# A graph network in two layers: the first node tables as a software pipeline, with one difference on GpSimd and the loads on three queues

## The chip, the cores and the metric

The kernel runs on one core of a Trainium2 chip. A core has five engines that run side by side, each through its own instructions in order: PE (TensorE, matrix products into PSUM), DVE (VectorE), ACT (ScalarE), POOL (GpSimd) and SP (SyncE, which here only issues transfers). An instruction that waits for another engine holds up everything behind it on its own. ACT and POOL can issue transfers too. The time is microseconds on the device, from start to end of one execution. It is the median of several executions.

## The reference, cut to what matters

There are 6250 nodes with 128 channels and 200,000 edges, sorted by `dst`. Two layers of attention over the edges follow each other, each with a residual and a layer norm.

```python
# layer 0: a score for each edge, a softmax over the edges of one src
hij = concatenate([x[src], x[dst]], -1)
e = leaky_relu(hij @ w, 0.2) @ a
att = exp(e) / segment_sum(exp(e), src)[src]
x = layernorm(x + segment_sum(x[src] * att, dst))
# layer 1: four heads, scores from two projections, sum into src, elu
s = leaky_relu(H_s[:, src] + H_t[:, dst]); s = exp(s - max(s))
agg = scatter_add(src, s / (denom[src] + eps) * H[dst]) + x @ residual_projection
x = layernorm(x + elu(agg))
```

The change concerns only the start of layer 0: `hij @ w` is `x[src] @ w_top + x[dst] @ w_bottom`, so both products are made once for each node (the node tables) and then picked for each edge.

## The kernel before

The 6250 nodes make NB = 49 blocks of 128. The edges are sorted into NB x NB buckets by the block of their `src` and of their `dst`; each bucket has 128 slots. The work runs in three stages.

**Score stage** (`score_edges`). It holds all that the change touches.
- Constants come first, and `load_ids(0)` (L556 to L565) loads the source and destination numbers of the first seven windows of edges: fourteen transfers on SP's queue, seven for `src` and then seven for `dst`.
- `find_slots(j)` (from L596) is a generator that finds the slots of the edges of destination block j. Each `next` on it issues one portion, eleven portions in all. In this document they are calls one to eleven. (1) For a chunk's first j, `split_ids` takes the ids apart on DVE and asks for the next chunk's ids; then ACT repeats one part along a new axis (`repeat`, L606). (2) DVE compares (`soh`, L612). (3) PE adds up with a stair matrix (L619), ACT copies the sum (`earlier`, L621) and repeats two more parts. (4) Two `count`s, each a group of matmuls into one PSUM tile (L629, L631) and a DVE product from it (L638). (5) Three more counts, two folds (L653), a reduction to `ranks` (L656), and an ACT spread of half the ranks (L661). (6) Two DVE products `vst` (L670). (7) A DVE comparison `at` (L676), the second ACT spread. (8) PE places the first half (L681), DVE compares the second. (9) PE places the second half. (10) DVE takes the slots to `cb` and `cols` (L698, L699). (11) PE transposes, ACT copies to `rb` (L704), SP writes `rows_jm` and `rows_im` to DRAM (L706, L707).
- The node tables are made for blocks b = 0 to 48 (L720 to L758). PE transposes the block of x (L745), ACT copies it to `xt` (L747), PE multiplies (`tables`, L729) into 128x260 values in PSUM. Then `split3` (L474 to L481) writes them as three bf16 parts to `pq3`: ACT rounds (`high`, L477), DVE subtracts (L479, tile `pqr`), ACT rounds the rest (L480), DVE subtracts again (`low`, L481). Transposes run one block ahead of the products; the four operations of `split3` come in a row. x comes in chunks of seven blocks into three buffers, on SP's queue. All PSUM tiles of this loop, those of `count` among them, come from one pool "u" of four.
- In the same loop three searches start at blocks 0, 12 and 24, and `find_more` moves each running search on by one portion after every second block.
- Behind it the pair loop goes over all 49 x 49 pairs of blocks (7 chunks of 7 for each j). It fetches slot rows, makes one-hot matrices of them on DVE (L793), multiplies them with `pq3` (L817), and takes the scores from PSUM on DVE (L827). The searches of the later j run between. Its buffers follow those of the table loop, in memory and in PSUM.

**Layer 0** and **layer 1** (`bucketed`) gather and sum with one-hot matrices (L1050, L1080; L1217, L1249).

The order on each engine is the order in which the program text issues the instructions; no planner changes it. POOL works only on constants at the start of the stages.

Of the kernel before, what the change touches and what calls it, by code (L numbers as in the profile page):

```python
# [8 lines left out]
F32 = mybir.dt.float32  # L9
# [3 lines left out]
AF = mybir.ActivationFunctionType  # L13
OP = mybir.AluOpType
AX = mybir.AxisListType

P = 128
# [457 lines left out]
def split3(nc, pool, hi, mid, lo, v, shape, name):  # L475

    nc.scalar.activation(hi, v, AF.Copy)  # L477
    r = pool.tile(shape, F32, name=name)
    nc.vector.tensor_tensor(r, v, hi, op=OP.subtract)  # L479
    nc.scalar.activation(mid, r, AF.Copy)  # L480
    nc.vector.tensor_tensor(lo, r, mid, op=OP.subtract)  # L481


def score_edges(tc, keep, x, src, dst, w0, a0, rows_jm, rows_im):
# [4 lines left out]
    nc = tc.nc  # L489
    N, C = x.shape  # L490
    (E,) = src.shape
    NB = -(-N // P)
    LAST = N - (NB - 1) * P
    NI = -(-NB // 2) * 2
    WT, starts = windows(N, E, NB)
    CX = C + 2
    CH = 7
    chunks = [(c, min(c + CH, NB)) for c in range(0, NB, CH)]
    NC = len(chunks)
    AHEAD = 3  # L500
# [7 lines left out]
    with ExitStack() as pools:  # L508
# [22 lines left out]
        ident = fc.tile([P, P], F32, name="ident")  # L531
# [5 lines left out]
        w0_sb = fc.tile([P, 2, CX], F32, name="w0_sb")  # L537
# [10 lines left out]
        part = ALPHA / (1.0 - ALPHA)  # L548
# [6 lines left out]
        ids, parts = {}, {}  # L555

        def load_ids(b):
            if b < NC:
                c0, c1 = chunks[b]
                ids[b] = [fi.tile([P, CH, WT], I32, name=f"ids{k}") for k in range(2)]  # L560
                for to, flat in zip(ids[b], (src, dst)):
                    for j in range(c0, c1):
                        nc.sync.dma_start(
                            to[:, j - c0, :], flat[starts[j] : starts[j] + WT * P].rearrange("(p t) -> p t", t=WT)
                        )  # L565

        def split_ids(b):


            load_ids(b + 1)  # L570
            c0, c1 = chunks[b]
            n = c1 - c0
            got = []
            for k, number in enumerate(ids.pop(b)):
                number = number[:, :n].rearrange(flat2)
                hl = fi.tile([P, 2, CH, WT], BF16, name=f"hl{k}")
                for h, (by, op) in enumerate(((7, OP.arith_shift_right), (P - 1, OP.bitwise_and))):
                    tmp = fi.tile([P, CH * WT], I32, name="tmp")
                    nc.vector.tensor_single_scalar(tmp[:, : n * WT], number, by, op=op)
                    nc.vector.tensor_scalar(  # L580
                        hl[:, h, :n].rearrange(flat2), tmp[:, : n * WT], 1.0, None, op0=OP.add
                    )
                got.append(hl)
            here = fi.tile([P, CH, WT], BF16, name="here")
            nc.vector.tensor_tensor(
                here[:, :n],
                got[1][:, 0, :n],
                iota_1[:, c0:c1, None].to_broadcast([P, n, WT]),
                op=OP.is_equal,
            )  # L590
            nc.vector.tensor_reduce(counts[:, b : b + 1], here[:, :n].rearrange(flat2), axis=AX.X, op=OP.add)
            nc.vector.tensor_tensor(got[0][:, 0, :n], got[0][:, 0, :n], here[:, :n], op=OP.mult)  # L592
            parts[b] = got[0][:, 0], got[0][:, 1], got[1][:, 1]
# [115 lines left out]
        finding, pa = [], []  # L709

        def find_more():
            for f in list(finding):
                if next(f, finding) is finding:
                    finding.remove(f)


        load_ids(0)
        pqp = pools.enter_context(tc.tile_pool(name="pq", bufs=1))
        pq3 = pqp.tile([P, NB, 2, 3, CX], BF16, name="pq3")
        with (  # L720
            tc.tile_pool(name="n0", bufs=3) as n0,
            tc.tile_pool(name="n0u", bufs=4, space=bass.MemoryType.PSUM) as n0u,
        ):
            pa[:] = [n0u]
            ahead, turned = iter(range(AHEAD)), []

            def tables(b, xt):
                mm = n0u.tile([P, 512], F32, name="u")[:, : 2 * CX].rearrange("p (w c) -> p w c", c=CX)
                nc.tensor.matmul(mm, xt, w0_sb, start=True, stop=True)  # L729
                split3(nc, n0, pq3[:, b, :, 0, :], pq3[:, b, :, 1, :], pq3[:, b, :, 2, :], mm, [P, 2, CX], "pqr")  # L730

            for c0, c1 in chunks:
                xc = n0.tile([P, CH, C], F32, name="xc")
                full = min(c1, NB - 1) if LAST < P else c1
                if full < c1:
                    nc.vector.memset(xc[:, full - c0, :], 0.0)
                    nc.sync.dma_start(xc[:LAST, full - c0, :], x[full * P :, :])
                if full > c0:
                    nc.sync.dma_start(
                        xc[:, : full - c0, :], x[c0 * P : full * P, :].rearrange("(b p) c -> p b c", p=P)  # L740
                    )
                for b in range(c0, c1):

                    tp = n0u.tile([P, 512], F32, name="u")[:, :P]
                    nc.tensor.transpose(tp, xc[:, b - c0, :], ident)  # L745
                    xt = n0.tile([P, P], F32, name="xt")
                    nc.scalar.activation(xt, tp, AF.Copy)  # L747
                    turned.append((b, xt))
                    if b > 0:
                        tables(*turned.pop(0))  # L750
                    if b % 12 == 0:
                        finding.extend(find_slots(j) for j in [next(ahead, None)] if j is not None)
                    if b % 2 == 0:
                        find_more()
            tables(*turned.pop(0))
            assert next(ahead, None) is None
            while finding:
                find_more()  # L758

# [40 lines left out]
        for k, (j, c) in enumerate(order):  # L800
# [7 lines left out]
            rows = loaded.pop(k)  # L808
            c0, c1 = chunks[c]
            for i0 in range(c0, c1, 3):  # L810
                n = min(3, c1 - i0)
                u = pa[0].tile([P, 512], F32, name="u")[:, : 3 * CX].rearrange("p (n c) -> p n c", c=CX)
                for d in range(n):
                    i = i0 + d
                    for w, b in ((0, i), (1, j)):
                        for s in range(3):
# [4 lines left out]
                                start=(w == 0 and s == 0),  # L821
                                stop=(w == 1 and s == 2),
# [8 lines left out]
            tp = ft.tile([P, CH, P], BF16, name="tp")  # L831
# [504 lines left out]
@with_exitstack  # L1336
def kernel(ctx, tc, x, src, dst, w0, a0, w1, al, ar, wr, out):
    nc = tc.nc
    ctx.enter_context(tc.manual_schedule())
    NB = -(-x.shape[0] // P)  # L1340
    keep = ctx.enter_context(tc.tile_pool(name="keep", bufs=1))
    dram = ctx.enter_context(tc.tile_pool(name="slots_d", bufs=1, space=bass.MemoryType.DRAM))
    rows_jm = dram.tile([NB, 2, NB, P], BF16, name="rows_jm")
    rows_im = dram.tile([NB, 2, NB, P], BF16, name="rows_im")
    cols, ok, ex, den = score_edges(tc, keep, x, src, dst, w0, a0, rows_jm, rows_im)
    fits = nc.values_load(
        ok, min_val=0, max_val=1, skip_runtime_bounds_check_because="a product of two comparisons is 0 or 1"
    )
    with tc.If(fits == 1) as cmp:
        bucketed(tc, x, w1, al, ar, wr, out, cols, ex, den, rows_jm, rows_im)  # L1350
    with cmp.Else():
        any_edges(tc, x, src, dst, w0, a0, w1, al, ar, wr, out)
# [35 lines left out]
```

## Time and profile before

| | |
|---|---|
| median of three runs | 4135.72 us (4134.61 to 4139.05) |
| the profiled execution | 4133.56 us |
| its span, first to last instruction | 4131.8 us |
| mean granted PE clock over the span | 0.957 of full speed |
| busy: PE, DVE, ACT, POOL | 3637.4, 3385.6, 2238.6, 1.7 us |
| first node table matmul (L745), last `low` (L481) | 11.71, 152.27 us |
| first fetch of slot rows issued, first pair matmul (L817) | 152.76, 158.18 us |
| end of the score stage, about | 1682 us |

Times inside the profile count from the first instruction. Each row of the time order names the start, the duration, the engine, the line of the program, the operation, the tile that it writes and those that it reads with their shapes; in brackets stands how long the engine had been idle before it, and what it waited for. In the list of waits the columns are the waiting engine and line, what it waited for, the total in microseconds, how many times, and the longest. The granted clock is the share of full speed that TensorE was given.

### The profile page before, as it was taken

The numbers are of one execution on the slowest core, as the hardware profiler recorded it, in microseconds if no ns is written. First come the engines' busy times: TensorE is split into PE (matmuls) and PEld (weight loads), VectorE is DVE, ScalarE is ACT, GpSimd is POOL, SyncE is SP. The second block draws the span as 40 slices with busy tenths as digits, with TensorE's granted clock in tenths as the row PEclk, the third lists the DMA queues.
The fourth block names the chain that finished last, engine by engine and source line by source line (L and its number), as shares of the span: only waits on it lengthen the run. The fifth ranks groups of instructions, "written<-read, shape, count | busy, mean of one in ns | idle before, by whom it ended". The sixth has DMA issues, their size and how long they took to land.

```text
span 4131.8 us, 133418 instructions
## 1 busy us (share of the span) xinstructions
PE 3637.4 (88%) x55225; PEld 3463.4 (84%) x55225; DVE 3385.6 (82%) x11437; ACT 2238.6 (54%) x3384; POOL 1.7 (0%) x12
## 2 busy tenths in 40 slices
PE   5788899898889889499999999997999999999982
PEld 3588888888888888399999999996999999999972
DVE  5688888888888888588788888876888888888886
ACT  5456555555555554234434434436666766666653
POOL 0000000000000000000000000000000000000000
PEclk7899999999999999699999999997999999999995
DMA  1233333333333333222322222224444444444431
GB/s 31 74 110 110 105 103 110 108 106 101 114 106 106 99 114 117 78 83 78 82 79 78 79 82 78 79 71 135 133 134 132 135 134 136 129 134 135 135 96 50
DMA packets 300811, 423.28 MB, mean 102 GB/s; under 512 B 53094, under 2 KB 298660, under 8 KB 300196
## 3 DMA queue, kind: packets, MB, share of 16 engines
q1 hardware_dynamic: 299204, 414.19, 33.3%
q8 instruction: 438, 7.18, 0.7%
q14 instruction: 177, 1.45, 0.1%
q10 hardware_dynamic: 992, 0.46, 0.0%
HBM read 405.66 MB, written 8.87 MB: 100 GB/s over the span
## 4 chain that ended last, share of the span: by engine, by line
PE 60%; DVE 28%; ACT 6%; issue 2%; DMA 2%; SPq 0%; DVEq 0%; ACTq 0%
PE oj L1080 13%; PE agg L1249 12%; PE ye L1050 9%; PE he L1217 9%; PE u L817 7%; DVE junk L827 5%; DVE at L676 3%; DVE rows L793 3%; ACT spread L661 3%; DVE r L638 2%; DVE vst L670 2%; PE sm L619 2%; DVE z L1228 1%; PE sp L1175 1%; DVE r L653 1%
## 5 line engine op out<-in xcount | busy, mean ns | idle before, releaser
L817 PE MATMUL u<-pq,rows 128*128 128x130 bf16 x14406 | 914.7, 221 | 104.1 <-DVE junk L827 96.3
L817 PEld LDWEIGHTS <-rows 128*128 128x128 bf16 x14406 | 851.1, 98 | 122.1 <-issue 116.7
L1062 DVE TENSOR_SCALAR oh<-iota_b,dsts,ex 128x128 f32<-128x128 bf16 x2401 | 658.1, 340 | 144.3 <-PE oj L1080 106.0
L1249 PE MATMUL agg<-z,oh 128*128 128x132 f32 x4802 | 700.6, 287 | 70.9 <-DVE oh L1235 70.9
L1080 PE MATMUL oj<-yc,oh 128*128 128x128 f32 x4802 | 691.3, 284 | 3.3 <-ACT yc L1058 2.9
L1249 PEld LDWEIGHTS agg<-z,oh 128*128 128x128 f32 x4802 | 601.9, 193 | 72.5 <-issue 60.1
L1058 ACT ACTIVATE yc<-ye 128x512 f32<-128x512 f32 (+1 forms) x686 | 370.6, 543 | 538.3 <-PE ye L1050 532.1
L827 DVE SCALAR_TENSOR_TENSOR junk<-u,a_ext 128x130 bf16<-128x130 f32 x2401 | 544.8, 286 | 105.6 <-PE u L817 104.2
L1080 PEld LDWEIGHTS oj<-yc,oh 128*128 128x128 f32 x4802 | 596.2, 193 | 5.2 <-ACT yc L1058 4.0
L1050 PE MATMUL ye<-y,rows 128*128 128x128 bf16 x7203 | 519.5, 220 | 76.9 <-DVE rows L925 76.9
L1050 PEld LDWEIGHTS <-rows 128*128 128x128 bf16 x7203 | 465.5, 99 | 93.2 <-issue 59.2
L1228 DVE TENSOR_TENSOR z<-he,z 128x512 f32<-128x512 f32 (+1 forms) x686 | 424.6, 619 | 135.6 <-ACT z L1225 83.0
L1217 PE MATMUL he<-h,rows 128*128 128x128 bf16 x7203 | 519.0, 220 | 0.0
L835 ACT ACTIVATE oh<-tp 128x896 bf16<-128x896 bf16 x343 | 311.8, 909 | 336.5 <-PE tp L833 334.5
L1217 PEld LDWEIGHTS <-rows 128*128 128x128 bf16 x7203 | 443.8, 98 | 6.5
L1235 DVE TENSOR_TENSOR oh<-iota_b,cols 128x512 f32<-128x512 bf16 (+1 forms) x686 | 420.5, 613 | 0.0
L920 ACT ACTIVATE rows<-rows,minus_p 128x896 bf16<-128x896 bf16 x343 | 352.3, 1027 | 1.6 <-DMA rows<-rows_im 1.6
L661 ACT ACTIVATE spread<-ranks 128x2816 bf16<-128x2816 bf16 x98 | 249.3, 2544 | 168.2 <-DVE ranks L656 168.2
L921 ACT ACTIVATE rows<-rows 128x896 bf16<-128x896 bf16 x343 | 325.9, 950 | 10.9
L606 ACT ACTIVATE spread<-hl 128x2200 bf16<-128x2200 bf16 x147 | 292.8, 2024 | 39.6 <-DVE hl L592 39.6
L925 DVE TENSOR_SCALAR rows<-rows,part_f 128x896 bf16<-128x896 bf16 x686 | 301.8, 446 | 12.9 <-DMA rows<-rows_im 9.2
L1225 ACT ACTIVATE z<-score,neg_c 128x16 f32<-128x16 f32 (+1 forms) x686 | 184.3, 296 | 220.4 <-PE agg L1249 153.6
(158 smaller groups left out, 3701.9 us busy)
## 6 DMA issues: line engine op xcount, KB each, us to landing
rows<-rows_jm SPq DMA_DIRECT2D x1029, 224.0 KB
rows<-rows_im SPq DMA_DIRECT2D x686, 224.0 KB
res_d<-rs SPq DMA_DIRECT2D x7, 448.0 KB
res<-res_d SPq DMA_DIRECT2D x7, 448.0 KB
xc<-in_x_dram SPq DMA_DIRECT2D x6, 448.0 KB
out_dram<-o SPq DMA_DIRECT2D x6, 448.0 KB
rows_jm<-rb SPq DMA_DIRECT2D x98, 12.2 KB
rows_im<-rb SPq DMA_DIRECT2D x98, 12.2 KB
```

The costliest lines, as they stand in the source:

```text
L661: nc.scalar.activation(rx, ranks[:, h * WH : (h + 1) * WH, None].to_broadcast([P, WH, P]), AF.Copy)
L817: nc.tensor.matmul(u[:, d, :], rows[:, w, i - c0, :], pq3[:, b, w, s, :], start=(w == 0 and s == 0), stop=(w == 1 and s == 2),)
L827: nc.vector.scalar_tensor_tensor(junk, u[:, d, :], 0.0, a_ext, op0=OP.max, op1=OP.mult, accum_out=acc[:, i : i + 1])
L920: nc.scalar.activation(rows, rows, AF.Square, bias=minus_p)
L1050: nc.tensor.matmul(ye[:, k, :], oh[:, i0 + k - c0, :], y3[:, i0 + k, s, :], start=(s == 0), stop=(s == 2))
L1058: nc.scalar.activation(yc[:, :n], ye[:, :n], AF.Copy)
L1062: nc.vector.tensor_scalar(oh[:, k, :], iota_b, dsts[0][:, i : i + 1], ex[:, j, i : i + 1], op0=OP.is_equal, op1=OP.mult,)
L1080: nc.tensor.matmul(outs[j], oh[:, k, :], yc[:, k, :], start=(i == 0), stop=(i == NB - 1))
L1217: nc.tensor.matmul(he[:, k, :], oh[:, j0 + k - c0, :], h3[:, j0 + k, s, :], start=(s == 0), stop=(s == 2))
L1228: nc.vector.tensor_tensor(z[:, :n, :C].rearrange("p n (h d) -> p n h d", h=H), he[:, :n].rearrange("p n (h d) -> p n h d", h=H), z[:, :n, ...
L1235: nc.vector.tensor_tensor(oh[:, :n], iota_b[:, None, :].to_broadcast([P, n, P]), cols[:, j0 : j0 + n, 0, i : i + 1].to_broadcast([P, n, P] ...
L1249: nc.tensor.matmul(aggs[i], oh[:, k, :], z[:, k, :], start=(j == 0), stop=(j == NB - 1))
```

## The change

The order of the table loop is turned into steps. At step t each operation works on another block: rest (the first difference) on block t-4, the copy of the transposed block on t-1, the transpose on t, the product on t-2, high on t-3, middle on t-5, low on t-6. They are issued in this order in every step, 55 steps in all. The copy (`keep_turned`) moves from ACT to DVE, the second difference (`low`) from DVE to POOL. The PSUM pool "u" of four becomes one of three for the tables and one of a single tile for the counts. x is loaded into four buffers instead of three, on POOL's queue and one to two chunks ahead; the first chunk's `dst` ids come on ACT's queue. Searches start at steps 0, 14 and 28, and of the running searches those at an even place in the list move on at even steps, the others at odd ones.

```diff
--- before.py
+++ after.py
@@ -558,9 +558,9 @@
             if b < NC:
                 c0, c1 = chunks[b]
                 ids[b] = [fi.tile([P, CH, WT], I32, name=f"ids{k}") for k in range(2)]
-                for to, flat in zip(ids[b], (src, dst)):
+                for to, flat, queue in zip(ids[b], (src, dst), (nc.sync, nc.scalar if b == 0 else nc.sync)):
                     for j in range(c0, c1):
-                        nc.sync.dma_start(
+                        queue.dma_start(
                             to[:, j - c0, :], flat[starts[j] : starts[j] + WT * P].rearrange("(p t) -> p t", t=WT)
                         )
 
@@ -718,42 +718,72 @@
         pqp = pools.enter_context(tc.tile_pool(name="pq", bufs=1))
         pq3 = pqp.tile([P, NB, 2, 3, CX], BF16, name="pq3")
         with (
-            tc.tile_pool(name="n0", bufs=3) as n0,
-            tc.tile_pool(name="n0u", bufs=4, space=bass.MemoryType.PSUM) as n0u,
+            tc.tile_pool(name="n0", bufs=4) as n0,
+            tc.tile_pool(name="n0u", bufs=3, space=bass.MemoryType.PSUM) as n0u,
+            tc.tile_pool(name="n0c", bufs=1, space=bass.MemoryType.PSUM) as n0c,
         ):
-            pa[:] = [n0u]
-            ahead, turned = iter(range(AHEAD)), []
-
-            def tables(b, xt):
-                mm = n0u.tile([P, 512], F32, name="u")[:, : 2 * CX].rearrange("p (w c) -> p w c", c=CX)
-                nc.tensor.matmul(mm, xt, w0_sb, start=True, stop=True)
-                split3(nc, n0, pq3[:, b, :, 0, :], pq3[:, b, :, 1, :], pq3[:, b, :, 2, :], mm, [P, 2, CX], "pqr")
-
-            for c0, c1 in chunks:
+            pa[:] = [n0c]
+            rows, tps, xts, mms, rests = {}, {}, {}, {}, {}
+
+            def load_rows(c):
+                c0, c1 = chunks[c]
                 xc = n0.tile([P, CH, C], F32, name="xc")
                 full = min(c1, NB - 1) if LAST < P else c1
                 if full < c1:
-                    nc.vector.memset(xc[:, full - c0, :], 0.0)
-                    nc.sync.dma_start(xc[:LAST, full - c0, :], x[full * P :, :])
+                    nc.gpsimd.memset(xc[:, full - c0, :], 0.0)
+                    nc.gpsimd.dma_start(xc[:LAST, full - c0, :], x[full * P :, :])
                 if full > c0:
-                    nc.sync.dma_start(
+                    nc.gpsimd.dma_start(
                         xc[:, : full - c0, :], x[c0 * P : full * P, :].rearrange("(b p) c -> p b c", p=P)
                     )
                 for b in range(c0, c1):
-
-                    tp = n0u.tile([P, 512], F32, name="u")[:, :P]
-                    nc.tensor.transpose(tp, xc[:, b - c0, :], ident)
-                    xt = n0.tile([P, P], F32, name="xt")
-                    nc.scalar.activation(xt, tp, AF.Copy)
-                    turned.append((b, xt))
-                    if b > 0:
-                        tables(*turned.pop(0))
-                    if b % 12 == 0:
-                        finding.extend(find_slots(j) for j in [next(ahead, None)] if j is not None)
-                    if b % 2 == 0:
-                        find_more()
-            tables(*turned.pop(0))
-            assert next(ahead, None) is None
+                    rows[b] = xc[:, b - c0, :]
+
+            def part(b, s):
+                return pq3[:, b, :, s, :]
+
+
+            def turn(b):
+                tps[b] = n0u.tile([P, 512], F32, name="u")[:, :P]
+                nc.tensor.transpose(tps[b], rows.pop(b), ident)
+
+            def keep_turned(b):
+                xts[b] = n0.tile([P, P], F32, name="xt")
+                nc.vector.tensor_copy(xts[b], tps.pop(b))
+
+            def multiply(b):
+                mms[b] = n0u.tile([P, 512], F32, name="u")[:, : 2 * CX].rearrange("p (w c) -> p w c", c=CX)
+                nc.tensor.matmul(mms[b], xts.pop(b), w0_sb, start=True, stop=True)
+
+            def high(b):
+                nc.scalar.activation(part(b, 0), mms[b], AF.Copy)
+
+            def rest(b):
+                rests[b] = n0.tile([P, 2, CX], F32, name="pqr")
+                nc.vector.tensor_tensor(rests[b], mms.pop(b), part(b, 0), op=OP.subtract)
+
+            def middle(b):
+                nc.scalar.activation(part(b, 1), rests[b], AF.Copy)
+
+            def low(b):
+                nc.gpsimd.tensor_tensor(part(b, 2), rests.pop(b), part(b, 1), op=OP.subtract)
+
+            load_rows(0)
+            load_rows(1)
+            stages = ((rest, 4), (keep_turned, 1), (turn, 0), (multiply, 2), (high, 3), (middle, 5), (low, 6))
+            first = [0, 14, 28]
+            assert len(first) == AHEAD
+            for t in range(NB + 6):
+                if t % CH == 1 and 1 < t // CH + 2 < NC:
+                    load_rows(t // CH + 2)
+                for stage, lag in stages:
+                    if 0 <= t - lag < NB:
+                        stage(t - lag)
+                if t in first:
+                    finding.append(find_slots(first.index(t)))
+                for k, f in enumerate(list(finding)):
+                    if t % 2 == k % 2 and next(f, finding) is finding:
+                        finding.remove(f)
             while finding:
                 find_more()
```

## The prediction

> **What bounds the stage that the change touches.** I first cut the span into stages by the engines' busy time (columns: stretch, its length, then busy time and count for PE, weight loads, DVE, ACT, POOL, the granted clock, DMA share, GB/s).
>
> ```profile
> core 0: us, PE busy (x) PEld busy (x) DVE busy (x) ACT busy (x) POOL busy (x), PEclk, DMA share, GB/s
> 0.00:7.50 7.50, 0.00 (x0) 0.00 (x0) 3.29 (x17) 1.28 (x1) 0.95 (x8) 1.00 0.32 62
> 7.50:152.80 145.30, 82.62 (x561) 52.01 (x561) 79.18 (x154) 77.91 (x168) 0.00 (x0) 0.69 0.10 26
> 152.80:1682.00 1529.20, 1369.37 (x25558) 1281.69 (x25558) 1338.99 (x6096) 848.76 (x812) 0.00 (x0) 0.99 0.35 108
> ```
>
> Only the first 152.8 us are touched: node tables and the first three slot searches. No engine is full there: DVE 79 of 145 us, ACT 78, PE 83 at a clock of 0.69. So it is bound by waits, and all that can be won lies between 145 us and some 80. The pair stage after it can't begin earlier than its end (the first pair matmul, L817, starts at 158.18), so a microsecond saved here is one off the end. The waits of this stretch, longest first:
>
> ```profile
> DVE pqr L479 <- ACT pq L477: 39.0, 15, 6.3
> ACT pq L480 <- DVE pqr L479: 35.2, 49, 2.8
> ...
> DVE pq L481 <- ACT pq L480: 23.8, 49, 0.5
> ACT xt L747 <- PE u L745: 20.7, 8, 9.3
> ACT spread L661 <- DVE ranks L656: 11.6, 3, 4.0
> ```
>
> ACT and DVE wait for each other, 49 times: one table's halves follow each other. In order of time, one block where no search is in the way:
>
> ```profile
> 40.21 0.26 ACT L747 ACTIVATE xt<-u 128x128 f32<-128x128 f32 x1
> 40.34 0.43 DVE L481 TENSOR_TENSOR pq<-pqr,pq 128x260 bf16<-128x260 f32 x1 [0.49 <-ACT pq L480]
> 40.44 0.39 ACT L477 ACTIVATE pq<-u 128x260 bf16<-128x260 f32 x1
> 40.52 0.50 PEld L729 LDWEIGHTS u<-w_sb,xt 128*128 128x128 f32 x2 [0.53 <-ACT xt L747]
> 40.52 1.23 PE L729 MATMUL u<-w_sb,xt 128*128 128x260 f32 x2
> 40.86 0.43 DVE L479 TENSOR_TENSOR pqr<-u,pq 128x260 f32<-128x260 f32 x1
> 41.12 0.23 PEld L745 LDWEIGHTS u<-ident,xc 128*128 128x128 f32 x1
> 41.32 0.42 ACT L480 ACTIVATE pq<-pqr 128x260 bf16<-128x260 f32 x1 [0.49 <-DVE pqr L479]
> 41.55 0.42 PE L745 MATMUL u<-ident,xc 128*128 128x128 f32 x1
> 41.65 0.26 ACT L747 ACTIVATE xt<-u 128x128 f32<-128x128 f32 x1
> ```
>
> From copy to copy (40.21 to 41.65) is **1.44 us**, of which ACT works about 1.0 and DVE 0.86.
>
> **Part 1, the block step.** In the new order rest works on block t-4 while copy, product, high and middle work on others, so no two operations of a step need each other except through the three "u" buffers. Bounds of a step:
> - DVE: rest 0.43 (the row above) and the copy. No row copies 128x128 f32 from PSUM on DVE; near are 0.23 (L541, same size, from SBUF) and 0.26 (L698, 128x100 from PSUM). I take 0.27: 0.70.
> - ACT: high 0.38 and middle 0.42: 0.80.
> - PE: transposes and products back to back start 1.1 us apart at the low clock (76.39 to 77.50) and 0.63 apart at the full one (92.88 to 93.51).
> - Buffers: a transpose takes the buffer that rest has freed. Product to high is 1.11 us at the low clock (54.45 to 55.56), 0.64 at the full one (93.07 to 93.71); high to rest 0.42; rest to transpose 0.48; transpose to product about 0.2. That is 2.2 or 1.75 us for two steps.
>
> So a step is 0.87 to 1.1 us; with the mixed clock seen (0.5 to 0.76 in slices of this stretch) 1.05. There are 55 steps instead of 49 blocks, the outer six partly empty: I count 52. Not all are exposed: under the long stalls of part 2 eighteen pass hidden, before and after. 31 x 1.44 = 44.6 becomes 34 x 1.05 = 35.7: **-9** (ends: 0, if a step stays 1.3; -17, if ACT's 0.80 is reached).
>
> **Part 2, the searches.** Each of three has three long stalls, and ACT and DVE run in order, so the tables wait behind them. From the second search: calls three (both repeats, 95.85 to 103.13: 7.3 us), four (two counts, to 107.6: 4.4) and five (three counts, ranks, a spread, to the vst product at 119.0: 11.4), 23.1 in all. New:
> - Call three: ACT still waits for the stair matmuls, then has 0.2 + 3.95; DVE and PE run one step ahead meanwhile, then need ACT's next high. About 7.6.
> - Counts: their PSUM tile was one of four; now it is one alone, so each count waits for DVE's product before it (0.67). In the old order two counts ran 26.24 to 29.42; in series 2 x (1.13 + 0.67) plus handovers, and rest, transpose, product ahead of them: about 6.1 for call four.
> - Call five: three such rounds to 6, then 1.18 + 0.8 + 0.2 of folding, spread 2.55, high 0.4: 10.8. The 1.6 us of ping-pong before vst go.
>
> Sum 24.5: **+4** for three (ends: -7, full clock; +11, low clock and no step hidden). Call six (vst, 2.5 us of DVE) took 5.0 to the next; DVE alone needs 2.5 + 1.4 = 3.9: **-3**.
>
> **Part 3, loads.** The first spread starts at 12.37, behind the table copy (12.20) that waits for x (landing 11.57) and the split, which waits for dst (8.91). On ACT's queue dst follows a_all and w0 (to 1.6), 7 x 0.45: issued by 4.9, landed by about 6.5, before DVE is through src (5.83 to 7.1). Split ends near 9.7, spread follows at once: **-2.7**. ACT computes nothing before that, so its issuing is covered; a first compute before 4.9 would pay. The x loads waited on SP behind the searches' writes. Two of these waits cost nothing: at 76.4 and 115 ACT was in a spread until 77.1 and 115.8. The third is bare (DVE's memset ends at 135.1, x lands at 139.66): **-4.6**. Loading one or two chunks ahead hides POOL's load. SP keeps the fourteen ids loads of chunk 1 and the searches' writes; nothing new waits there.
>
> **Part 4, GpSimd.** POOL has 49 differences, eight loads and a memset. No row shows it with two inputs. Nearest is its 128x128 select, 0.29 us with one: times 260/128 is 0.59. GPSIMD Engine Reference of the Trainium skill, section 3.1, puts two-input work at some 2.6 cycles an element: an estimate of 0.56 at its 1.2 GHz before dispatch, 0.84 by its measured ratio of 1.96 to DVE's 0.43. I take 0.8 (0.43 to 1.7), 39 us in all, off the path: rest of block b waits only for low of b-4, two steps back. How long a load of 896 rows holds POOL is not shown; from SP's 0.4 to several us, I take 1.5, covered by that slack.
>
> Against the change speaks SBUF — State Buffer, section "Who interferes with whom": a DVE instruction with two SBUF inputs and a GpSimd instruction that reads SBUF exclude each other for the whole instruction. The trace, with POOL idle throughout, shows nothing of it: by the rows alone the cost is 0. By the rule 21 instructions of the searches (soh, r twice, vst twice, at twice, for three) may find POOL at work and wait up to 0.8: 17 at most. POOL is busy about three tenths of the time, half an operation is left on average, and waiting for ACT often hides it: **+3**.
>
> The last low ends the stage; on POOL it takes 0.8 for 0.43: **+0.4**.
>
> **Sum:** -9 + 4 - 3 - 2.7 - 4.6 + 3 + 0.4 = -11.9. The profiled execution took 4133.56 (span 4131.8 and 1.8 around it), so 4121.7. The median shown is 4135.72, 2.2 higher, and times are compared with it: **4123.5**. The stage would end near 141.
>
> **Rivals.**
> - *The lag swallows the searches.* If ACT's backlog and DVE's folding overlap as well as a six-block lag suggests, the stage nears what its fullest engine needs: DVE 78 (49 x 0.7, three searches of 12.5, 4 of split, constants), with a third of waits about 105 from 9.7 on. End at 115, -38: 4098. For it: no engine is full. Against: rest needs high one step later, not four; only low is truly late. Chance 0.22.
> - *The counts and locks take it back.* Low-clock counts (+11), locks 8, a step of 1.15: -5 + 11 + 8 - 3 - 7.3 + 0.4 = +4, and with half of these locks and counts -5: 4131 to 4140, centre 4134. For it: clock 0.5 to 0.7 after each ACT spread. Chance 0.18: no change.
> - *GpSimd becomes the clock, slower.* Rest waits for low four blocks back. Today's average is 141 us for 49 blocks, 2.9 each; as soon as low plus a seventh of a load exceeds that, POOL sets the pace. At low 1.7 and loads of 12 us it is 3.4 x 49 = 167: +26, 4160. Against: the 0.29 us row. Chance 0.06.
> - *Not what it says:* the pair stage could wait for another thing than the tables. The first row load was issued at 152.76, just after the last low at 152.27, so the tables free it. I leave nothing for this.
>
> **How the numbers follow.** My forecast has 0.54, its own range 4115 to 4130. Faster by over 0.2% means under 4127.4 (what a measurement here can tell from no change is about 8 us): most of the forecast (0.5), the first rival and a little of the second: 0.74. Same: 0.19. Slower: 0.07. The range takes in most of the first rival and the near part of the second: 4099 to 4134.
>
> **What would show it.** Right: L817 first starts near 146; the x waits are gone; ACT's 49 waits for DVE fall from 35 us to under 10; POOL shows 49 operations of about 0.8. Counts: r's wait for PE rises by some 1 us per cut. Locks: soh, vst or at longer than 1.30 and 1.62 while POOL works. Wrong: steps outside the searches still 1.4 apart, or rest waiting for POOL, or a stretch after 158 that is no longer the same length.

## The result, and the profile after

| | before | after |
|---|---|---|
| median of twelve runs | 4135.12 us (4132.84 to 4139.05) | 4136.76 us (4133.97 to 4140.03) |
| ratio, 95% interval | | 1.0003 (0.9994 to 1.0012) |
| profiled execution, span | 4133.56, 4131.8 us | 4138.26, 4136.5 us |
| first ACT spread (L606) | 12.37 us | 15.20 us |
| first fetch of slot rows issued | 152.76 us | 151.60 us |
| first pair matmul (L817, now L847) | 158.18 us | 156.22 us |
| pair stage, first to last pair matmul | 1518.6 us | 1523.7 us |

No change that can be measured; 4123.5 was forecast. In the changed kernel the table loop's lines are: rest L763, `keep_turned` L752, turn L748, multiply L756, high L759, middle L766, low L769, the x loads L734 and L736. Lines behind the loop are 30 higher. First the engines' busy time by stretches of the changed kernel, with the columns of the same view before.

```profile
0.00:7.50 7.50, 0.00 (x0) 0.00 (x0) 2.49 (x13) 0.00 (x0) 3.84 (x11) 1.00 0.65 176
7.50:151.60 144.10, 83.33 (x561) 52.11 (x561) 72.79 (x157) 66.55 (x120) 44.32 (x55) 0.67 0.09 21
```

The work moved as the change says: ACT fell from 77.9 to 66.6 us, DVE from 79.2 to 72.8, and POOL has 44.3. The granted clock (0.67 after 0.69) and PE's busy time (83.3 after 82.6) are nearly the same. The stretch is hardly shorter (144.1 us after 145.3), and no engine is near its length. So there are new waits. They are read from the list of waits of this stretch in the changed kernel:

```profile
PE u L748 <- DVE pqr L763: 41.4, 23, 4.2
ACT pq L759 <- PE u L756: 38.1, 26, 4.7
DVE pqr L763 <- ACT pq L759: 37.6, 19, 6.1
DVE r L638 <- PE u L631: 22.7, 15, 2.7
ACT spread L661 <- DVE ranks L656: 21.0, 3, 7.5
```

ACT's 35.2 us for the middle part are gone, as forecast. What stands in their place is a ring: the transpose waits for rest (41.4), high waits for the product (38.1), rest waits for high (37.6). The two last lines are the searches: `r` waits for its matmuls 22.7 us where it did not wait before, and the spread waits for the ranks 21.0 instead of 11.6.

The start, in order of time in the changed kernel:

```profile
1.61 2.93 POOL L736 DMA_DIRECT2D xc<-in_x_dram  x3
1.64 8.15 ACTq L563 DMA_DIRECT2D ids<-in_dst_dram  x7
...
11.61 0.32 DVE L579 TENSOR_SCALAR tmp<-ids 128x308 int32<-128x308 int32 x1 [5.96 <-DMA ids<-in_src_dram]
...
15.20 2.04 ACT L606 ACTIVATE spread<-hl 128x2200 bf16<-128x2200 bf16 x1 [4.09 <-DVE hl L592]
```

The same places in the kernel before:

```profile
5.83 0.32 DVE L579 TENSOR_SCALAR tmp<-ids 128x308 int32<-128x308 int32 x1
...
7.59 0.43 SPq L739 DMA_DIRECT2D xc<-in_x_dram  x1
...
12.37 2.03 ACT L606 ACTIVATE spread<-hl 128x2200 bf16<-128x2200 bf16 x1
```

x is asked for at 1.61, at the same moment as the `dst` ids; before it was asked for at 7.59, behind all ids. DVE starts to split the `src` ids at 11.61; before it started at 5.83.

### The profile page after: what moved, and what is told of

Read it like the earlier page. It is cut to its first block, busy times and chain, and to the rows that moved or that the text cites. A ratio compares the mean times of both kernels' runs of the same rounds, so it can differ in the third digit from the quotient of the medians.

```text
span 4136.5 us, 133397 instructions
## 1 busy us (share of the span) xinstructions
PE 3637.3 (88%) x55225; PEld 3462.8 (84%) x55225; DVE 3380.6 (82%) x11436; ACT 2226.6 (54%) x3335; POOL 48.9 (1%) x70
## 4 chain that ended last, share of the span: by engine, by line
PE 60%; DVE 29%; ACT 6%; issue 3%; DMA 2%; SPq 0%; DVEq 0%; POOL 0%; ACTq 0%
PE oj L1110 13%; PE agg L1279 12%; PE he L1247 9%; PE ye L1080 9%; PE u L847 7%; DVE junk L857 6%; DVE at L676 3%; DVE rows L823 3%; ACT spread L661 3%; DVE r L638 2%; PE sm L619 2%; DVE vst L670 2%; PE sp L1205 1%; DVE r L653 1%; PE u L631 1%
## 5 line engine op out<-in xcount | busy, mean ns | idle before, releaser
L847 PE MATMUL u<-pq,rows 128*128 128x130 bf16 x14406 | 915.0, 221 | 105.1 <-DVE junk L857 97.6
L847 PEld LDWEIGHTS <-rows 128*128 128x128 bf16 x14406 | 851.7, 98 | 123.0 <-issue 109.7
L606 ACT ACTIVATE spread<-hl 128x2200 bf16<-128x2200 bf16 x147 | 292.8, 2024 | 43.7 <-DVE hl L592 43.7
L955 DVE TENSOR_SCALAR rows<-rows,part_f 128x896 bf16<-128x896 bf16 x686 | 303.7, 449 | 13.5 <-DMA rows<-rows_im 10.2
```

The source lines that it names most:

```text
L847: nc.tensor.matmul(u[:, d, :], rows[:, w, i - c0, :], pq3[:, b, w, s, :], start=(w == 0 and s == 0), stop=(w == 1 and s == 2),)
```

## The experiments

Two accounts were open. One is the start, which came 2.8 us late instead of 2.7 early. The other is the loop: from the first spread to the first fetch it took 136.4 us after 140.4, where the other terms of the forecast made about 131. Each diff is against the changed kernel and cut to what matters, and times before the change are those of the same chip. "Stage end" is the issue of the first slot row fetch. Most variants ran once; how far single executions differ is told at the end of this section.

**The start: which of the two moved loads is it?** The next two put back one half each.

*x behind the ids, on SP's queue for the first two chunks:*

```diff
-            load_rows(0)
-            load_rows(1)
+            load_rows(0, nc.sync)
+            load_rows(1, nc.sync)
```

> The first two chunks of x are issued on SP's queue, behind the ids, as before; all else as in the changed kernel, dst on ACT's queue too. Theory A (x, issued at 1.61 us on GpSimd's queue, fills the DMA engines just when the small ids loads need them): the first spread starts between 10 and 12.5 us instead of 15.20, and the first pair matmul between 151 and 154 instead of 156.22. Rival (it is the second issuing queue for the ids that slows them): first spread still after 14 us, first pair matmul within 1 us of 156.2.

First spread 13.48, stage end 149.28, whole 4134.54 (before: 4133.36).

*The dst ids back on SP, x left on POOL's queue:*

```diff
-                for to, flat, queue in zip(ids[b], (src, dst), (nc.sync, nc.scalar if b == 0 else nc.sync)):
+                for to, flat, queue in zip(ids[b], (src, dst), (nc.sync, nc.sync)):
```

> All ids of the first chunk are issued on SP's queue, x stays on GpSimd's. Theory A (x in front of the ids is the cause): the first spread stays at 15 us or later. Rival (two queues for the ids are the cause): it starts near 12.4 as before, and the first pair matmul near 153.

First spread 14.04, stage end 149.86, whole 4134.59. So neither theory holds alone: each half gives back 1.2 to 1.7 us and stays later than before the change. Each rests on one execution; of the kernels that keep the whole changed start, three reach the first spread at 14.92, 15.20 and 15.24, and one at 17.03. Why x hurts is seen in the transfers. The windows from 4 to 8 us, the kernel before first and then the changed one (the last two columns are DMA share and GB/s):

```profile
4.00:8.00 4.00, 0.00 (x0) 0.00 (x0) 2.42 (x11) 0.00 (x0) 0.00 (x0) 1.00 0.32 50
```

```profile
4.00:8.00 4.00, 0.30 (x2) 0.33 (x3) 1.59 (x7) 0.00 (x0) 0.54 (x1) 1.00 1.00 291
```

The first three x loads, 448 KB each, fill the DMA engines just when the ids, 22 KB each, must pass. With the ids on SP and x still early, the share in that window is 1.01 and both splits come late (8.63 and 11.63, instead of 5.83 and 8.91). Why the second queue helps little is seen in the issuing, in the run with x behind first and then before the change:

```profile
0.74 4.60 SPq L563 DMA_DIRECT2D ids<-in_src_dram  x7
...
1.64 5.88 ACTq L563 DMA_DIRECT2D ids<-in_dst_dram  x7
```

```profile
0.74 3.48 SPq L563 DMA_DIRECT2D ids<-in_src_dram  x7
...
4.27 3.27 SPq L563 DMA_DIRECT2D ids<-in_dst_dram  x7
```

The fourteen ids loads of the first chunk are issued by 7.5 from two queues, and by 7.5 from SP alone. In the run with x behind, the third chunk of x still goes out on POOL's queue at 1.60; beside that same load SP alone needs until 7.9 and 8.2 (the next two runs). So two queues gain 0.4 to 0.7 us of issuing, and the seven `src` loads, which DVE needs first, take 4.60 us instead of 3.48.

*Both put back* was run twice, the second time with thirteen executions:

> Both halves of the new start are undone: all ids of the first chunk on SP's queue and the first two chunks of x behind them, on SP's queue too; the rest of the changed kernel stays. Theory A, as the two runs before left it (x and the second queue each cost some 1 to 2 us, and add): first spread between 11 and 12.5 us instead of 15.20, first pair matmul between 151.5 and 153.5 instead of 156.22. Rival (either of the two alone is enough, nothing is added): first spread at 13.5 to 14 as with one of them, first pair matmul near 154.3.

> The version of e5_start, timed against the kernel before: the changed kernel with ids and first x as before. If a microsecond of the table stage is one of the whole, as the first pair matmul (151.05 against 158.18) says: a ratio near 0.9983, 4128 us. Rival (the rest of the program gives it back): ratio 0.9993 to 1.0005.

First spread 11.73 and 12.06, stage end 146.35 and 147.32. The timed one has a median of 4133.34 (4130.80 to 4136.94), ratio 0.9993 (0.9985 to 1.0002) to before. Its first split and spread:

```profile
7.76 0.32 DVE L579 TENSOR_SCALAR tmp<-ids 128x308 int32<-128x308 int32 x1 [2.12 <-DMA ids<-in_dst_dram]
...
12.06 2.04 ACT L606 ACTIVATE spread<-hl 128x2200 bf16<-128x2200 bf16 x1 [9.14 <-DVE hl L592]
```

So the moved loads explain the late start: together they cost 3.1 to 3.5 us at the first spread, about the sum of the halves, and the stage ends 4.3 to 5.3 us earlier without them. The first split still starts later than before (7.46 and 7.76 after 5.83), with the third chunk of x ahead of the ids; the spread is not late for it, since it no longer waits for the table copy. The ratio to before is 0.9993 after 1.0003, with an interval that still holds no gain: the 0.9983 that was forecast from the first pair matmul did not come, and the rival's 0.9993 did.

**The loop: one tile for two uses?** In the order of the program, exactly three tables' tiles are in use after each step: the transpose of block t, the products of t-2 and t-3. The next transpose takes the tile that rest has just freed. On PE, behind that transpose, stand the product, and through it high and rest. In the changed kernel, in order of time around ACT's two repeats of a search:

```profile
23.01 3.95 ACT L606 ACTIVATE spread<-hl 128x2200 bf16<-128x2200 bf16 x2
26.86 0.37 ACT L759 ACTIVATE pq<-u 128x260 bf16<-128x260 f32 x1
...
27.26 0.43 DVE L763 TENSOR_TENSOR pqr<-u,pq 128x260 f32<-128x260 f32 x1 [6.12 <-ACT pq L759]
...
27.74 0.48 PE L748 MATMUL u<-ident,xc 128*128 128x128 f32 x1 [4.18 <-DVE pqr L763]
```

ACT is away for 3.95 us, then high runs; DVE had waited 6.12 for it, and PE's transpose had waited 4.18 for DVE. One engine's absence stops the other two. To test this, transpose and product got columns of their own in the same three tiles:

```diff
-                tps[b] = n0u.tile([P, 512], F32, name="u")[:, :P]
+                tps[b] = us[b % 3][:, 2 * CX : 2 * CX + P]
...
-                mms[b] = n0u.tile([P, 512], F32, name="u")[:, : 2 * CX].rearrange("p (w c) -> p w c", c=CX)
+                mms[b] = us[b % 3][:, : 2 * CX].rearrange("p (w c) -> p w c", c=CX)
```

> The three PSUM tiles of the tables are split by columns: block b has the product in columns 0 to 259 and its transpose in 260 to 387 of tile b mod 3, so that a transpose waits for the copy three blocks back instead of for rest four blocks back. Theory B (the three shared tiles tie each transpose to rest of the same step, so that the lag of six blocks is worth about one step): PE's wait for rest falls from 41 us to under 15 and the first pair matmul comes between 140 and 150 instead of 156.22. Rival (the searches' own waits, in order on ACT and DVE, set the pace whatever the buffers): the wait only changes its name, first pair matmul within 3 us of 156.2.

Stage end 131.67, 19.9 us earlier than in the changed kernel; first pair matmul 136.47, beyond the forecast of 140 to 150; whole 4118.28 against 4133.36 before. In its list of waits there is none of a transpose for rest any more. A part of that wait has a new name, as the rival said: the product waits for the copy. The longest between tables and searches:

```profile
PE u L757 <- DVE xt L753: 31.7, 20, 6.8
DVE pqr L764 <- ACT pq L760: 29.1, 12, 6.6
...
ACT pq L760 <- PE u L749: 18.0, 15, 3.6
DVE r L638 <- PE u L631: 14.5, 13, 1.7
```

And in its order of time PE goes on under the repeats:

```profile
59.54 3.95 ACT L606 ACTIVATE spread<-hl 128x2200 bf16<-128x2200 bf16 x2
...
60.57 0.38 PE L749 MATMUL u<-ident,xc 128*128 128x128 f32 x1
60.57 0.41 PEld L757 LDWEIGHTS u<-w_sb,xt 128*128 128x128 f32 x2
60.78 0.61 PE L757 MATMUL u<-w_sb,xt 128*128 128x260 f32 x2
...
61.23 0.27 PE L749 MATMUL u<-ident,xc 128*128 128x128 f32 x1
```

The tie is shown: it is the largest loss in the changed loop that a single edit removed. From the first spread to the stage end it is 116.8 us instead of 136.4. The granted clock was higher too (0.71 after 0.65 in that stretch), so some of this may be the clock's, but the gain comes again with the old start: 113.8 us with split tiles (a run below) and 134.6 and 135.3 without. Nearly half of the gain lies within calls three to five (from the stair matmul to `vst`: 65.8 us for the three searches, 74.8 in the changed kernel), the rest between them.

**The counts: is it their single tile?** One shared pool of four, as before the change:

```diff
-            tc.tile_pool(name="n0u", bufs=3, space=bass.MemoryType.PSUM) as n0u,
-            tc.tile_pool(name="n0c", bufs=1, space=bass.MemoryType.PSUM) as n0c,
+            tc.tile_pool(name="n0u", bufs=4, space=bass.MemoryType.PSUM) as n0u,
...
-            pa[:] = [n0c]
+            pa[:] = [n0u]
```

> The changed kernel with tables and counts in one PSUM pool of four tiles, as before, instead of three and one. If the single count tile costs what the prediction gave it (some 1.5 us a search), and a fourth tile lets transposes run one allocation further ahead, the first pair matmul comes 4 to 10 us before 156.2, and DVE's wait for the counts falls from 23 to about 10 us. Rival (counts now take tiles from the tables in turn and stop transposes): no gain, within 3 us of 156.2.

First spread 15.24, stage end 145.89 (-5.7), whole 4130.68 against a median of 4136.2 before. From its list of waits:

```profile
PE u L755 <- DVE pqr L762: 33.5, 17, 4.1
DVE r L638 <- PE u L631: 21.5, 15, 2.6
PE u L629 <- DVE r L638: 6.9, 9, 0.8
```

The counts stayed in series: `r` waits for PE 21.5 us, after 22.7, and the next count waits for `r` nine times, as in the changed kernel. So the pool of its own is not what puts them in series. With three tables' tiles in use, a pool of four leaves one for the counts, as the pool of one did; that follows from the program, and no run gave the counts a second tile. The 5.7 us are one execution at a higher clock (0.70 after 0.65 from the first spread on); what the list shows for them is in the tables, whose transposes wait for rest 33.5 us instead of 41.4.

**The locks and GpSimd.** Locks are here the times in which DVE and GpSimd keep each other waiting. The second difference back on DVE, with nothing else changed:

```diff
-                nc.gpsimd.tensor_tensor(part(b, 2), rests.pop(b), part(b, 1), op=OP.subtract)
+                nc.vector.tensor_tensor(part(b, 2), rests.pop(b), part(b, 1), op=OP.subtract)
```

> The second difference goes back from GpSimd to DVE. Theory C (exclusion of DVE's two-input operations and GpSimd costs what it lengthens them by): vst is back at 1.30, at at 1.62, soh at 1.30 us, 3.4 us less in sum, and the first pair matmul comes 2 to 4 us before 156.2, if DVE's own 49 x 0.43 us fall into its waits. Rival (DVE is near enough to the path that the move was worth its price): first pair matmul 3 to 15 us later than 156.2.

First spread 17.03, stage end 151.76, whole 4137.51. The start came 1.8 us later still, which nothing in the edit explains. The groups of the first 160 us, `vst` and `at`, first of the changed kernel, then with the difference on DVE (count, busy time, mean ns):

```profile
L670 DVE TENSOR_TENSOR vst<-soh,spread 128x2200 bf16<-128x2200 bf16 x6 | 9.6, 1638 | 0.0
L676 DVE TENSOR_TENSOR at<-spread,iota 128x2816 bf16<-128x2816 bf16 x6 | 10.4, 1741 | 0.0
```

```profile
L670 DVE TENSOR_TENSOR vst<-soh,spread 128x2200 bf16<-128x2200 bf16 x6 | 7.5, 1297 | 0.0
L676 DVE TENSOR_TENSOR at<-spread,iota 128x2816 bf16<-128x2816 bf16 x6 | 9.7, 1620 | 0.0
```

No row of them is longer without a difference running on POOL. With `soh` (1297 to 1462 ns) the three lines gain 3.3 us (6 x 0.34, 6 x 0.12, 3 x 0.17). It goes both ways, as the order of time of the changed kernel shows:

```profile
88.11 3.96 POOL L769 TENSOR_TENSOR pq<-pqr,pq 128x260 bf16<-128x260 f32 x3 [9.58 <-ACT pq L766]
...
88.37 3.20 DVE L670 TENSOR_TENSOR vst<-soh,spread 128x2200 bf16<-128x2200 bf16 x2
```

Three lows took 3.96 us where three alone take 1.9 (0.64 each), beside two `vst` that took 3.20 instead of 2.51. In the version with single counts (below) it is POOL alone that pays: its `vst`, `at` and `soh` keep 1.29 to 1.63 us, beside lows of up to 2.11.

*What is moving it to GpSimd worth?* With tied tiles, nothing that shows: from the first spread to the stage end the changed kernel takes 136.4, this run 134.7. The same comparison was made with split tiles and the old start, low on POOL and then on DVE:

> The start of the run before, and the tables' three PSUM tiles split by columns. If start and buffers are separate causes: first pair matmul at 136.5 less what the start alone gave, so 132 to 134, and the whole near 4114. Rival (the shorter start only moves the wait to the next long stall): first pair matmul within 1 us of 136.5.

> As the run before, with the second difference on DVE instead of GpSimd. With the transposes free, DVE is the fullest engine (72 of 124 us). Theory: now the move to GpSimd is worth something, and taking it back costs 3 to 10 us against the run before. Rival (the exclusion of the two engines costs as much as the move saves, as it did with the tied buffers): within 2 us of it.

Stage ends 125.38 and 131.18, whole 4111.68 and 4118.01 (before: 4132.97). From first spread to stage end they take 113.8 and 118.6 us. DVE's busy time in it is 69.0 and 80.8 us, so the sign fits the theory. But the granted clock was 0.75 and 0.68 and PE's busy time 72.5 and 78.5, and two executions of one program differ by more than 4.7 us (below). So that the move pays once the tiles are split is likely from these two runs and not shown.

**The counts issued one by one.** In the changed order a `next` hands over two or three counts at once, and each waits for `r` with the tables behind it. With split tiles and the old start, each count became a portion of its own, as did the spread, and every running search moves on after every step:

```diff
-            for cut in cuts[:2]:
+            for k, cut in enumerate(cuts):
                 count(*cut)
-            yield
-            for cut in cuts[2:]:
-                count(*cut)
+                if j < AHEAD or k == 1:
+                    yield
...
+            if j < AHEAD:
+                yield
             rx = spread(0)
...
-                    if t % 2 == k % 2 and next(f, finding) is finding:
+                    if next(f, finding) is finding:
```

> As the run with the split tiles and the old start, and the searches of the table stage are issued in fifteen portions instead of eleven: each count by itself, and the first spread of the ranks one portion after them; each running search moves on in every step. Theory (what is left are the in-order waits inside a search: ACT for the ranks 19 us, DVE for a count 14 us, PE for DVE's product 12 us; table steps put between them fill these waits): those three waits fall to under 25 us in sum and the first pair matmul comes 5 to 15 us earlier than with the split tiles and the old start. Rival (with all of a search in fifteen steps instead of 22 the other stalls come closer together): no gain, or up to 8 us later.

> The version of e8_counts_fine, timed against the kernel before: split tiles, ids and first x as before, counts issued one by one. By its one look (first pair matmul at 117.4 against 158.2): a ratio of 0.990 to 0.993, 4096 to 4106 us.

The first has its stage end at 112.67 and a whole of 4100.48. The second is the same kernel, timed: stage end 102.86, median 4090.86 us (4087.20 to 4097.74, four runs), ratio 0.9893 (0.9878 to 0.9909). That is 45 us below before, whose median there was 4136.2, and better than forecast. Its longest waits between tables and searches, from the timed kernel's list up to the stage end:

```profile
ACT pq L761 <- PE u L750: 14.0, 15, 1.4
PE u L758 <- DVE xt L754: 13.2, 9, 2.2
DVE r L638 <- PE u L631: 10.7, 9, 3.9
DVE pqr L765 <- ACT pq L761: 5.5, 8, 1.5
ACT spread L660 <- DVE ranks L655: 4.9, 3, 1.6
```

Against the changed kernel `r` waits half as long, the spread a quarter, rest a seventh. Against the run with split tiles and the old start, in the first of the two profiles, the spread waits for the ranks 3.1 us instead of 18.6, and PE's wait for `r` (13.1) is gone, while `r` waits for its matmuls as long as there (14.8 after 13.5). In sum that is 17.9 us after 45.2, and under 25 was forecast. The finer portions and the faster pace came in one edit; which of them does more was not tried.

**The spread of single executions.** The kernel before, profiled again:

> The kernel before, unchanged, for a second profile. In its first profile the pair stage lasts 1518.6 us from first to last pair matmul, in the changed kernel 1523.7, and in the other variants 1519.9 to 1523.9. Theory (that is the spread of single executions): this profile has 1519 to 1525. Rival (the changed table stage leaves something behind that slows the pair stage): again 1518 to 1519. The table stage itself should be the same to within 1 us: first spread at 12.4, first pair matmul at 158.2.

Stage end 151.62 (152.76 in the first), pair stage 1521.3 us (1518.6). So two executions of one kernel differ by 1.1 us here and 2.7 there. In all kernels with a changed table loop the pair stage took 1519.9 to 1524.3. From the first pair matmul to the end of the span it is 3973.6 and 3977.3 us in the two profiles of before, and 3977.9 to 3981.6 in all others. So the whole gains some microseconds less than the table stage does, and the prediction's "a microsecond saved here is one off the end" holds only to within these. Whether the rest is longer for a reason, or by chance, stays open: there are only two values of before.

## Why the prediction was wrong, term by term

The stage end moved by -1.2 us where -11.9 was summed (against the second profile of before, by nothing). Two steps failed: the start, and the block step under the searches' stalls. The terms as the profile of after has them:

| term | forecast | measured | from |
|---|---|---|---|
| start, to the first spread | -2.7 | +2.8 | 12.37 to 15.20 |
| bare wait for x | -4.6 | -4.6 | none left after the start |
| calls three to five, three searches | +4 | +4.8 | 69.9 to 74.8, stair matmul to first `vst` |
| block step, call six, locks, last low | -8.6 | -4.2 | what remains: 65.9 to 61.6 |

**The start failed as a step.** "Landed by about 6.5, before DVE is through src" priced the `dst` loads on ACT's queue by SP's 0.45 each and left x out of the transfers. x had waited on SP's queue behind the ids, and that place was their protection. The experiments show both halves: x fills the DMA engines (share 1.00 after 0.32 from 4 to 8 us), and the seven `dst` loads on ACT's queue took 8.15 us to issue in the changed kernel, and still 5.88 with x behind, where 7 x 0.45 was taken. The error is 5.5 us, the largest of the table.

**The block step failed in its sum, not in its price.** 1.05 us was forecast for a step. Where nothing is in the way it takes 0.91 to 0.99, by three starts of rest in the changed kernel:

```profile
61.08 0.42 DVE L763 TENSOR_TENSOR pqr<-u,pq 128x260 f32<-128x260 f32 x1
61.55 0.33 PE L748 MATMUL u<-ident,xc 128*128 128x128 f32 x1 [0.17 <-DVE pqr L763]
...
61.99 0.42 DVE L763 TENSOR_TENSOR pqr<-u,pq 128x260 f32<-128x260 f32 x1
...
62.98 0.43 DVE L763 TENSOR_TENSOR pqr<-u,pq 128x260 f32<-128x260 f32 x1 [0.36 <-ACT pq L759]
```

The prediction saw that "a transpose takes the buffer that rest has freed" and priced that for an undisturbed step only. It is the disturbed step where it costs. From a search's first `vst` to the next one's stair matmul it was 15.1 us twice, with six blocks in it; now it is 18.2 and 16.0, with eight steps. Six times 1.44 leaves 6.4 us for the search's pieces before; eight times 0.95 leaves 10.6 and 8.4 now, of which locks are about 1.1. With split tiles it is 16.1 and 12.6, which leaves 8.5 and 5.0. So, counted this way, the steps became cheaper and the pieces between them dearer by nearly as much, since with the tie hardly more than a step runs beside a piece. The tie costs 19.9 us by the experiment, more than the 4.4 that this row lacks: without it the loop takes 116.8 us from the first spread to the stage end, where about 131 were forecast.

**The searches were priced about right.** Calls three to five were forecast at 7.6, 6.1 and 10.8; in the second search they took 8.2, 6.4 and 10.4. (The rows of before from 95.85 to 119.0, called the second search's, are the third's, with 23.1 us; the second took 23.6. The parts given for call five add to 11.1, and -11.9 from 4135.72 is 4123.8, not 4123.5. Neither changes the outcome.) The wait of `r` for PE rose by 1.5 us a count (some 1 was named). But the reason for the counts was incomplete: without their pool of one they stay in series too. Call six took 4.3 (3.9). **The locks** were forecast at 3, and the rows are longer by 3.3 in sum; what of it lies on the path is not shown. **low** was forecast at 0.8 and is 0.83 in the mean; a load on POOL holds it 0.94 us (1.5 taken).

**The rival with the swallowed searches** was set aside because "rest needs high one step later, not four". The runs don't bear that out as the limit: with the same lags, split tiles and counts issued one by one, the stage ends at 102.9 to 112.7. What kept the lag from working was the tile, and then the lumps or the pace in which the searches come. No rival named the tile. The no-change rival has the right time and partly wrong reasons: calls three to five took 4.8 us, the late start 2.8, and the tie, which it does not name, can account for what the cheaper step did not bring.

## What to carry to other kernels

For each rotating buffer of a software pipeline, count how many are in use between two steps. If all are, as here, the lag between the operations can be worth one step only, however many blocks lie between them; test it with the longest stall in the loop, not with the plain step. A large load that is moved to a free queue can come ahead of the small ones that the start waits for: before moving it, look at what its old place kept it behind.

## What was not expected of the hardware

**A second queue issued the small loads hardly faster.** With one x load ahead, fourteen loads of 22 KB had been issued by 7.9 and 8.2 us from SP alone, and by 7.5 from SP with ACT.

**Two executions of one program differed by 10 us in this stage, and the granted clock with them.** The kernel with single counts was profiled twice, on two chips, with stage ends at 112.67 and 102.86, although its first spread started at 11.64 and 11.98. A stretch of each and the whole from the first spread to the stage end, first the later one (the third number from the right is the granted clock):

```profile
50.00:70.00 20.00, 15.19 (x85) 9.31 (x85) 14.97 (x30) 13.15 (x23) 9.31 (x11) 0.57 0.08 23
...
11.64:112.67 101.03, 78.77 (x561) 51.64 (x561) 65.86 (x146) 64.69 (x119) 44.45 (x55) 0.70 0.11 27
```

```profile
50.00:70.00 20.00, 14.65 (x107) 9.67 (x108) 17.05 (x37) 13.89 (x26) 12.68 (x16) 0.83 0.11 35
...
11.98:102.86 90.88, 67.65 (x561) 43.92 (x561) 65.84 (x146) 64.53 (x119) 45.38 (x55) 0.85 0.12 29
```

DVE and ACT are busy equally long in both, with the same number of instructions; PE needs 78.8 us for its 561 at a clock of 0.70, and 67.7 us at 0.85. Why the clock differs between the two is not known from these runs, nor whether the chip matters. It is the limit of all single profiles of this stage: differences of a few microseconds between two of them are not read as effects here, unless a wait shows them too.
